# Layer 0 of a two-layer convolution and attention kernel: image sums, image loads and spectra steps in another place

## The chip, the cores and the metric

One core of a Trainium2 chip runs the whole kernel. A core has TensorE (matrix products, PE in the profile, its weight loads PEld), VectorE (DVE), ScalarE (ACT), GpSimd (POOL) and SyncE (SP, here only issuing DMAs), each with its own stream of instructions, joined by semaphores. The metric is the device time of one execution in microseconds, lower is better: the median of several runs. Everything is float32.

## The reference, cut to what matters

The input is x, 4 x 32 x 128 x 128: four "images" b, each of T = 32 planes of 128 x 128. Two layers follow each other; the change touches layer 0 alone.

```python
x = x + conv_attention(group_norm(x))       # layer 0
t = tokens(x)                               # layer 1
t = t + attention(layer_norm(t)); t = t + experts(layer_norm(t))

def conv_attention(x, ...):                 # planes xa = x.reshape(B*T, 1, H, W)
    xn = inorm(xa)                          # mean and variance of each plane
    k, q, v = fno(xn, K..), fno(xn, Q..), fno(xn, V..)   # 32 heads each
    p_attn = softmax(k and q over the T planes)
    p = fno(p_attn applied to v, P..)
    a = inorm(p + xa); an = inorm(a)
    m = gelu(inorm(spectral_conv(an)) + skip(an))
    m = inorm(spectral_conv(m)) + skip(m)
    return inorm(m) + a
```

`fno` is a spectral convolution (a 2-D FFT cut to 64 x 33 or 64 x 17 modes, a complex product for each mode, and the FFT back) plus a scaled copy of its input. `group_norm` takes mean and variance over groups of columns of a whole image, `inorm` over one plane. Both therefore need sums over all of an image before its spectra can be scaled.

## The kernel before, in words

**Staging.** Layer 0 keeps an image in SBUF as 128 partitions by 32 planes by 128 columns. FFTs are products with constant cosine and sine matrices. The loop `for b in range(B)` (L687) runs the back half of image b and, inside it, the front half of image b+1. Its stages in order of time are:

1. the load of image b+1 (`load`, L122, called at L692): four DMAs of 512 KB, two issued from SP and two from ACT;
2. the modes, `for x0 in range(0, KX, NK)` (L751): five chunks of up to 13 mode columns. For each chunk, SP broadcasts `xb` from DRAM (L758, eight DMAs, four buffers), DVE and POOL multiply (`u`, L775 and L773), PE sums into `po` (L778). The skip products `sk` (L742) are spread among them, and ACT copies a chunk out (`rs`, L788);
3. the way back to planes (`py` L798, `four` L278), and `spectra(0, q)`: by groups of GI = 8 planes, a first step `pz` (L248), copies to `z` (`evacuate`, L188 on ACT and L190 on DVE), the second step `px` (L871);
4. the first scale chain, `weighed("v0", ...)`: energies on DVE end in `v_s` (L915), a product with ones gives `ms` (L314), and a chain of small DVE and ACT operations gives `r0`, `hq`, `hs0`, `hb`;
5. `back` (L288) for two halves of the planes: `y` (L297), copies `v`, `four` (L308), and for each plane a DVE operation (L941), a GELU on ACT (L944) and its statistics (L951);
6. `image_sums` of image b+1 (L320): squares on ACT, row sums `rows8` on PE (L330, the profile's `rows`), a copy `ev`, `s12` (L343, the profile's `s`), then a DVE chain with three more small products, `mg`, `bg`, `my` (`sums`, L314), to the group norm's and the plane norm's scales `gn_r`, `colg`, `n_r`, `n_s`;
7. `spectra(1, gl)` and `spectra_of_images(b+1)` (L418): `forward` (L253) calls `first_step` (L243, `pz`), then `less_mean` (L433) takes the mean off columns 0 and 128 of `z`, then the second step `px` (L263, L264) and its scaling copy `xx` (L429);
8. the second scale chain, `attention_weights(b+1)` (L487): `so` (L503), `sod` (L506), products `pa` and `pb` on DVE (L522) and POOL (L524), `sp` (L528), the scores `sc` (L540, L547), a softmax;
9. the end of image b: ACT scales `gl` (L999), POOL adds it (L1006), DVE adds `four` (L1010), SP stores (L1016).

Before the loop, a startup does stages 6 to 8 for image 0, beside `value_weights` (L462, DVE operations L469 to L479) and other weights.

**What sets the order.** In layer 0 the tile framework's scheduler fixes the order of instructions on each engine from the program and from priorities; each engine then works strictly through its list. `tc.keep_in_program_order` and `tc.add_manual_dep` constrain it. Tiles of one tag share a fixed number of buffers. PSUM has the tags `a`, `b` and `wide`, two buffers each: `pz` and `po` are of tag `a`; `px`, `py` and `four` of `b`; `y`, `m`, `so`, `sc` and, before, all products of the image sums of `wide`. Layer 1's order is written out elsewhere and depends only on layer 0's end.

**Tables.** GELU and the logarithm with the exponential lie in two sets of ScalarE's tables, and a set is loaded when the function of another comes (`ACT_TABLE_LOAD` in the profile). `inv_std` (L204) takes a logarithm (L208) and an exponential (L209) for each inverse square root, and improves the result by a Newton step (L210 to L213). `logarithms()` (L129) loads the second set ahead of need.

Of the kernel before, what the change touches and what calls it, by code (L numbers as in the profile page):

```python
# [7 lines left out]
F32 = mybir.dt.float32  # L8
AF = mybir.ActivationFunctionType
ALU = mybir.AluOpType  # L10
# [3 lines left out]
P = 128  # L14
B, T, H, C = 4, 32, 128, 128
# [3 lines left out]
GI = 8  # L19
# [60 lines left out]
NK = 13  # L80
# [28 lines left out]
def layer0(  # L109
    tc, x, kq_modes, kq_mirror, vcw, pcw, mcols, mcol0, mrows, heads, heads_row, small_row, by_p, inv_cols, dram, x1, first  # L110
):
    nc = tc.nc
# [7 lines left out]
    const, ps, images, values, modes = (p.__enter__() for p in pools + right)  # L120

    def load(b):  # L122
        xt = images.tile([P, T, C], F32, name=f"x_{b}", tag="x")
        for g in range(0, T, GI):
            eng = nc.sync if g % 16 == 0 else nc.scalar
            eng.dma_start(out=xt[:, g : g + GI], in_=x[b, g : g + GI].rearrange("t w c -> w t c"))
        return xt
# [5 lines left out]
    loaded = load(0)  # L133
# [118 lines left out]

    def forward(images, c1, c2, take, change):  # L253


        n = c1.shape[1]
        z = grp.tile([P, GI, 192], F32, name="z", tag="z")
        first_step(images, z)
        change(z)
        for k in range(0, GI, 4):  # L260
            px = ps.tile([P, 4, n], F32, name="px", tag="b")
            for j in range(4):
                nc.tensor.matmul(px[:, j], z[:, k + j, :P], c1, start=True, stop=False)  # L263
                nc.tensor.matmul(px[:, j], z[:, k + j, 64:], c2, start=False, stop=True)  # L264
            take(k, px)
# [15 lines left out]
    GROUPS = range(0, T, GI)  # L281
# [28 lines left out]

    def sums(name, matrix, src):

        m = ps.tile(list(src.shape), F32, name=name, tag="wide")
        nc.tensor.matmul(m, matrix, src, start=True, stop=True)  # L314
        return m

    def one(name, n=1):
        return small.tile([P, n], F32, name=name, tag=name)

    def image_sums(b, xt):  # L320


        rows8 = ps.tile([64, 4, C], F32, name="rows8", tag="wide")
        for g in GROUPS:
# [13 lines left out]
        nc.scalar.copy(ev, rows8)  # L338
        s12 = ps.tile([P, 2, 512], F32, name="s12", tag="wide")[:, :, :T]
        for j in range(4):  # L340
            for k in range(2):
                r = slice(32 * k, 32 * k + 8)
                nc.tensor.matmul(s12[:, k, j::4], ev[r, j], ident[r, r], start=True, stop=True)  # L343
        sv = small.tile([P, 2, T], F32, name="sv", tag="pk_sq")
        nc.vector.tensor_copy(sv, s12)

        tot = one("tot", 2)
        nc.vector.tensor_reduce(tot, sv, AX.X, ALU.add)
        mg = sums("mg", group, tot)
        gm = one("gm")  # L350
# [11 lines left out]
        by_group = small.tile([P, 2, 32], F32, name="by_group", tag="by_group")  # L362
        nc.vector.tensor_copy(by_group, sums("bg", ones, both))
        n = 1 + 2 * KY
        colg = small.tile([P, 2, n], F32, name="colg", tag="colg")
        nc.vector.tensor_scalar(colg[:, 0], cols1[:, :n], gr, None, ALU.mult)
        nc.vector.tensor_scalar(colg[:, 1], cols2[:, :n], gr, None, ALU.mult)
        m128 = one("m128")
        nc.vector.tensor_scalar(m128, gm, 128.0, None, ALU.mult)

# [14 lines left out]
        nc.vector.tensor_scalar(y12, y12, 1.0 / NPIX, None, ALU.mult)  # L385
        my = sums("my", ones, y12)
        ym, yv = per_image("ym"), per_image("yv")
# [4 lines left out]
        ysc = scalars(ALU.mult, "n1_s", yr, par[:, N1W : N1W + 1])  # L392
        return by_group, colg, m128, ysc

# [23 lines left out]
    def spectra_of_images(b, xt, normed):  # L418


        _, colg, m128, ysc = normed
        n = 1 + 2 * KY
        xx = modes.tile([P, T, n], F32, name=f"xx_{b}", tag="xx")
        xd = dram.tile([T, 2, KX, KY], F32, name=f"xd_{b}")
        for g in GROUPS:

# [5 lines left out]

            def less_mean(z):  # L433
                nc.vector.tensor_scalar(z[:, :, 0], z[:, :, 0], m128, None, ALU.subtract)
                nc.vector.tensor_scalar(z[:, :, P], z[:, :, P], m128, None, ALU.add)

            forward([xt[:, g + t] for t in range(GI)], colg[:, 0], colg[:, 1], scaled, less_mean)

# [248 lines left out]
    for b in range(B):  # L687
        xt = loaded
        by_group, _, _, ysc = normed
        xd = front[2]  # L690
        if b + 1 < B:
            loaded = load(b + 1)  # L692

        ph, pr = weights
# [56 lines left out]
        for x0 in range(0, KX, NK):  # L751
# [3 lines left out]
            for i in range(4):  # L755
                xb = late.tile([P, 2, NK * KY], F32, name="xb", tag="xb")[:, :, :m]
                for r in range(2):
                    nc.sync.dma_start(  # L758
                        out=xb[:, r],
                        in_=xd[8 * i : 8 * i + 8, r, x0 : x0 + nk]  # L760
                        .rearrange("s x y -> s (x y)")
                        .unsqueeze(1)
                        .to_broadcast([8, 16, m]),
                    )
# [20 lines left out]
                if i % 2 and at_c < C:  # L785
                    skips(at_c)
                    at_c += 16
            nc.scalar.copy(rs[:, x0 : x0 + nk].rearrange("p x y -> p (x y)"), po)  # L788
        if b + 1 == B:
            for p in reversed(right):  # L790
                p.__exit__(None, None, None)
# [141 lines left out]
        nc.vector.tensor_mul(dq, dq, hs0)  # L933
        nc.vector.tensor_tensor(hb, hb, dq, ALU.add)
        gl = big.tile([P, T, C], F32, name=f"g_{b}", tag="y")
        st = grp.tile([P, T, 6], F32, name="st", tag="st")
# [20 lines left out]
        logarithms()  # L957
        if b + 1 < B:
            normed = image_sums(b + 1, loaded)
        else:  # L960
            first((ps, images))
# [684 lines left out]
```

## Time and profile before

| | |
|---|---|
| median of 3 runs | 3180.41 us (3179.98 to 3183.43) |
| the profiled execution | 3191.62 us, its span 3189.9 us |
| mean granted TensorE clock in it | 0.953 |
| busy share PE, DVE, ACT, POOL | 92%, 72%, 72%, 66% |
| layer 0, then layer 1 | 0 to about 1105 us, then to the end |
| `ms` of the first scale chain, b = 0, 1, 2 | 228.57, 486.75, 755.85 us |
| end of the last GELU | 256.8, 521.5, 783.6 us |
| end of `px` L871 of `spectra(1)` | 277.0, 543.5, 805.6 us |
| start of `so` (startup, then b = 0, 1, 2) | 66.8; 306.5, 572.6, 835.8 us |

How to read it: busy time is the union of the instructions of an engine; `PEclk` is the clock that the throttle granted TensorE, in tenths of full speed. In a timeline a row gives start, duration, engine, line, instruction, the tile written and the tiles read, their shapes and the count; the bracket is the engine's idle time before the row and who released it. A float32 product of TensorE mostly shows as two records. The chain of waits follows the work that ended last back from the last instruction. All line numbers are those of the kernel before.

### The profile page before, as it was taken

What the parts mean: (1) busy time and instruction counts of PE and PEld (TensorE: products, weight loads), DVE (VectorE), ACT (ScalarE), POOL (GpSimd) and SP (SyncE); (2) the same over time, 40 slices, a digit from 0 to 9 for tenths busy, and PEclk for the clock granted to TensorE, in tenths of its full rate; (3) what the DMA queues carried; (4) which work ended last, traced back from release to release, by engine and by line L of the source; (5) the groups of instructions that cost most, each with busy time, mean ns of one, the idle gap of its engine ahead of it and who ended that gap; (6) DMA issues with size and microseconds to landing.
All of it is one profiled execution on the core that took longest, in us unless ns stands there. A gap on an engine that the chain in (4) does not pass through costs nothing.

```text
span 3189.9 us, 53099 instructions
## 1 busy us (share of the span) xinstructions
PE 2928.7 (92%) x19634; PEld 1438.2 (45%) x19634; DVE 2290.9 (72%) x5035; ACT 2311.7 (72%) x3138; POOL 2102.7 (66%) x1831
## 2 busy tenths in 40 slices
PE   7888798798888789999999999999999999999997
PEld 5366365345546444444344443444444444444443
DVE  5876666667677566777666868866778777687887
ACT  2344243253343589998999999998999999999992
POOL 1621540460451289878788797889878889888773
PEclk6998998899898799999999999999999999999998
DMA  6301310130140211010111010011010011101000
GB/s 140 111 18 30 95 50 3 49 123 1 30 130 2 57 31 31 8 31 7 31 37 24 14 24 14 8 39 31 23 29 9 14 37 24 37 1 31 14 14 14
DMA packets 152308, 112.77 MB, mean 35 GB/s; under 512 B 36878, under 2 KB 140657, under 8 KB 151441
## 3 DMA queue, kind: packets, MB, share of 16 engines
q1 hardware_dynamic: 136209, 103.61, 12.2%
q10 hardware_dynamic: 15840, 5.77, 0.8%
q8 instruction: 155, 2.54, 0.3%
q14 instruction: 104, 0.85, 0.1%
HBM read 68.37 MB, written 20.00 MB: 28 GB/s over the span
## 4 chain that ended last, share of the span: by engine, by line
PE 61%; POOL 12%; ACT 9%; DVE 9%; issue 7%; DMA 1%; ACTq 0%; POOLq 0%; DVEq 0%; SPq 0%
PE d L1446 19%; PE po L1465 11%; PE px L1352 6%; ACT r L1496 4%; PE po L778 4%; PE n L1446 3%; POOL e L1505 3%; POOL e L1504 3%; PE pz L248 2%; PE four L308 2%; ACT e L1512 2%; PE px L871 1%; PE sk L742 1%; POOL kx L1111 1%; DVE r L1501 1%
## 5 line engine op out<-in xcount | busy, mean ns | idle before, releaser
L1501 DVE TENSOR_TENSOR r<-n,r 128x1024 f32<-128x1024 f32 (+1 forms) x1056 | 961.6, 952 | 479.0 <-PE n L1446 389.4
L1504 POOL TENSOR_TENSOR e<-r 128x512 f32<-128x512 f32 x528 | 673.2, 1275 | 268.1 <-DVE r L1501 267.6
L1496 ACT ACTIVATE r<-d 128x1024 f32<-128x1024 f32 (+1 forms) x1056 | 792.9, 802 | 67.4 <-PE n L1446 56.4
L1508 ACT ACTIVATE r<-r 128x1536 f32<-128x1536 f32 x528 | 783.6, 1484 | 16.8
L1505 POOL TENSOR_TENSOR e<-e,r 128x512 f32<-128x512 f32 x528 | 671.3, 1271 | 41.4
L1446 PE MATMUL d<-qe,ke 32*128 32x512 f32 (+3 forms) x2304 | 605.8, 602 | 39.6 <-ACT r L1496 36.5
L1465 PE MATMUL po<-e,kx 128*128 128x512 f32 (+3 forms) x1152 | 594.5, 605 | 15.6 <-POOL e L1517 15.6
L1446 PE MATMUL n<-qe,ke 32*128 32x512 f32 (+3 forms) x2304 | 606.2, 601 | 0.0
L1446 PE MATMUL n<-qf,kf 32*128 32x512 f32 (+3 forms) x2304 | 552.6, 554 | 0.0
L1446 PE MATMUL d<-qf,kf 32*128 32x512 f32 (+3 forms) x2304 | 550.2, 553 | 0.0
L1356 DVE SCALAR_TENSOR_TENSOR xc<-px,wgt,xc 128x128 f32<-128x128 f32 x1024 | 358.1, 350 | 42.2 <-PE px L1352 9.7
L1512 ACT ACTIVATE e<-e 128x512 f32<-128x512 f32 x528 | 325.8, 617 | 66.2 <-POOL e L1505 65.6
L1465 PEld LDWEIGHTS po<-e,kx 128*128 128x128 f32 x1152 | 175.5, 188 | 392.8 <-issue 306.9
L1446 PEld LDWEIGHTS d<-qe,ke 32*128 32x128 f32 x2304 | 176.5, 183 | 359.3 <-ACT r L1496 339.5
L773 POOL TENSOR_TENSOR u<-xb,gb 128x858 f32<-128x858 f32 (+1 forms) x120 | 233.1, 1968 | 139.5 <-PE po L778 128.0
L1446 PEld LDWEIGHTS d<-qf,kf 32*128 32x128 f32 x2304 | 220.2, 186 | 176.1 <-issue 163.8
L1352 PE MATMUL px<-we,x2t 128*128 128x512 f32 x512 | 264.0, 601 | 6.8 <-DVE xc L1356 6.0
L775 DVE TENSOR_TENSOR u<-xw,gb 128x858 f32<-128x858 f32 (+1 forms) x200 | 206.6, 1082 | 59.2 <-PE po L778 46.6
L885 POOL TENSOR_TENSOR spec<-part,part 128x512 f32<-128x512 f32 x16 | 24.8, 1550 | 333.4 <-ACT z L188 75.2
L1446 PEld LDWEIGHTS n<-qf,kf 32*128 32x128 f32 x2304 | 228.3, 185 | 19.2 <-issue 11.4
L778 PE MATMUL po<-u,pr 128*32 128x429 f32 (+1 forms) x1280 | 191.1, 548 | 26.8 <-DVE u L775 11.7
L524 POOL TENSOR_TENSOR pb<-xm 128x1024 f32<-128x1024 f32 x48 | 90.7, 1913 | 159.1 <-ACT xm L457 152.8
(388 smaller groups left out, 3953.9 us busy)
## 6 DMA issues: line engine op xcount, KB each, us to landing
xb<-xd SPq DMA_DIRECT2D x128, 214.5 KB
xc<-x SPq DMA_DIRECT2D x29, 512.0 KB
x<-x SPq DMA_DIRECT2D x16, 512.0 KB
qf<-qe SPq DMA_DIRECT2D x64, 128.0 KB
out<-xc SPq DMA_DIRECT2D x15, 512.0 KB
xb<-xd SPq DMA_DIRECT2D x32, 198.0 KB
gb<-gd SPq DMA_DIRECT2D x4, 1056.0 KB
x<-in_x SPq DMA_DIRECT2D x8, 512.0 KB
```

The costliest lines, as they stand in the source:

```text
L773: nc.gpsimd.tensor_tensor(u, xb, gk, ALU.mult)
L778: nc.tensor.matmul(po[32 * j : 32 * j + 32], pr[:, i, k], u[:, r], start=i == 0 and k == 0, stop=i == 3 and k == 1,)
L1352: nc.tensor.matmul(px, x2t[:, k * P : (k + 1) * P], we[:, e0 : e0 + 4], start=True, stop=True)
L1356: nc.vector.scalar_tensor_tensor(xc[:, k], px[:, e], wgt[:, k, e0 + e : e0 + e + 1], xc[:, k], ALU.mult, ALU.add)
L1446: nc.tensor.matmul(o, k, q, start=turn == 0 or g > 0, stop=turn == 1 or g > 0)
L1465: nc.tensor.matmul(sums[c, h][:, q0 : q0 + c1 - c0], kx[:, jb], e[:, c0:c1], start=jb == 0, stop=is_last and q0 > 2 * P, skip_group_check= ...
L1496: nc.scalar.activation(r[:, g], d, AF.Ln, scale=1.0 / DSCALE)
L1501: nc.vector.tensor_tensor(r[:, g], part, r[:, g], ALU.mult)
L1504: nc.gpsimd.tensor_tensor(e, r[:, 1], r[:, 2], ALU.add)
L1505: nc.gpsimd.tensor_tensor(e, e, r[:, 0], ALU.add)
L1508: nc.scalar.activation(r, r, AF.Exp, scale=-1.0)
L1512: nc.scalar.activation(e, e, AF.Exp)
```

## The change

It has four parts, with one consequence for allocation.

- `load` takes an instruction `behind`; for images 1 to 3 it is called after chunk 2 of the modes (`x0 == NK`). All four DMAs are issued from SP, ordered behind that chunk's last broadcast.
- `image_sums(b + 1)` is called right after `hb`, before the two `back` halves with the GELUs, not after them. Its products use the PSUM tags `a` and `b` instead of `wide`; `s12` becomes two tiles, copied by two operations.
- In `spectra_of_images`, `first_step` of the next group of planes is issued before `forward` of this one.
- The mean is taken off `z` by one operation on its columns 0 and 128 (`shift`, two values) instead of two (`less_mean`).

```diff
--- before.py
+++ after.py
@@ -119,11 +119,20 @@
     ]
     const, ps, images, values, modes = (p.__enter__() for p in pools + right)
 
-    def load(b):
+    def load(b, behind=None):
         xt = images.tile([P, T, C], F32, name=f"x_{b}", tag="x")
         for g in range(0, T, GI):
-            eng = nc.sync if g % 16 == 0 else nc.scalar
-            eng.dma_start(out=xt[:, g : g + GI], in_=x[b, g : g + GI].rearrange("t w c -> w t c"))
+            eng = nc.sync if behind is not None or g % 16 == 0 else nc.scalar
+            d = eng.dma_start(
+                out=xt[:, g : g + GI], in_=x[b, g : g + GI].rearrange("t w c -> w t c")
+            )
+            if behind is not None:
+                tc.add_manual_dep(
+                    d.ins,
+                    behind.ins.name,
+                    mybir.DependencyInfo(mybir.DependencyClass.NoSync, mybir.DependencyReason.DATA),
+                    reason="order",
+                )
         return xt
 
     def logarithms():
@@ -250,13 +259,10 @@
             if z.shape[2] > P:
                 evacuate(z[:, k : k + 4, P:], pz[:, :, :64], -1.0)
 
-    def forward(images, c1, c2, take, change):
+    def forward(z, c1, c2, take):
 
 
         n = c1.shape[1]
-        z = grp.tile([P, GI, 192], F32, name="z", tag="z")
-        first_step(images, z)
-        change(z)
         for k in range(0, GI, 4):
             px = ps.tile([P, 4, n], F32, name="px", tag="b")
             for j in range(4):
@@ -308,9 +314,9 @@
             nc.tensor.matmul(four, inv, v, start=True, stop=True)
             take([image(a, g, k) for k in range(4)], four)
 
-    def sums(name, matrix, src):
-
-        m = ps.tile(list(src.shape), F32, name=name, tag="wide")
+    def sums(name, matrix, src, tag="wide"):
+
+        m = ps.tile(list(src.shape), F32, name=name, tag=tag)
         nc.tensor.matmul(m, matrix, src, start=True, stop=True)
         return m
 
@@ -320,7 +326,7 @@
     def image_sums(b, xt):
 
 
-        rows8 = ps.tile([64, 4, C], F32, name="rows8", tag="wide")
+        rows8 = ps.tile([64, 4, C], F32, name="rows8", tag="a")
         for g in GROUPS:
             xx2 = grp.tile([P, GI, C], F32, name="xx2", tag="pr", bufs=6)
             nc.scalar.activation(xx2, xt[:, g : g + GI], AF.Square)
@@ -336,17 +342,18 @@
                     )
         ev = grp.tile([64, 4, C], F32, name="ev", tag="v", bufs=3)
         nc.scalar.copy(ev, rows8)
-        s12 = ps.tile([P, 2, 512], F32, name="s12", tag="wide")[:, :, :T]
+        s12 = [ps.tile([P, T], F32, name=f"s{t}", tag=t) for t in "ab"]
         for j in range(4):
             for k in range(2):
                 r = slice(32 * k, 32 * k + 8)
-                nc.tensor.matmul(s12[:, k, j::4], ev[r, j], ident[r, r], start=True, stop=True)
+                nc.tensor.matmul(s12[k][:, j::4], ev[r, j], ident[r, r], start=True, stop=True)
         sv = small.tile([P, 2, T], F32, name="sv", tag="pk_sq")
-        nc.vector.tensor_copy(sv, s12)
+        for k in range(2):
+            nc.vector.tensor_copy(sv[:, k], s12[k])
 
         tot = one("tot", 2)
         nc.vector.tensor_reduce(tot, sv, AX.X, ALU.add)
-        mg = sums("mg", group, tot)
+        mg = sums("mg", group, tot, "a")
         gm = one("gm")
         nc.vector.tensor_copy(gm, mg[:, 0:1])
         gv = one("gv")
@@ -360,13 +367,14 @@
         nc.vector.tensor_scalar(both[:, 0], of_group, gr, None, ALU.mult)
         nc.vector.tensor_scalar(both[:, 1], of_group, gs, -1.0, ALU.mult, ALU.mult)
         by_group = small.tile([P, 2, 32], F32, name="by_group", tag="by_group")
-        nc.vector.tensor_copy(by_group, sums("bg", ones, both))
+        nc.vector.tensor_copy(by_group, sums("bg", ones, both, "a"))
         n = 1 + 2 * KY
         colg = small.tile([P, 2, n], F32, name="colg", tag="colg")
         nc.vector.tensor_scalar(colg[:, 0], cols1[:, :n], gr, None, ALU.mult)
         nc.vector.tensor_scalar(colg[:, 1], cols2[:, :n], gr, None, ALU.mult)
-        m128 = one("m128")
-        nc.vector.tensor_scalar(m128, gm, 128.0, None, ALU.mult)
+        shift = one("shift", 2)
+        for k in range(2):
+            nc.vector.tensor_scalar(shift[:, k : k + 1], gm, 256.0 * k - 128.0, None, ALU.mult)
 
         gs128 = one("gs128")
         nc.vector.tensor_scalar(gs128, gs, 128.0, None, ALU.mult)
@@ -383,14 +391,14 @@
             y12[:, 1], sv[:, 0], grs, y12[:, 1], ALU.mult, ALU.add
         )
         nc.vector.tensor_scalar(y12, y12, 1.0 / NPIX, None, ALU.mult)
-        my = sums("my", ones, y12)
+        my = sums("my", ones, y12, "a")
         ym, yv = per_image("ym"), per_image("yv")
         nc.vector.tensor_copy(ym, my[:, 0])
         nc.vector.tensor_mul(yv, ym, ym)
         nc.vector.tensor_tensor(yv, my[:, 1], yv, ALU.subtract)
         yr, _ = inv_std("n1_r", yv)
         ysc = scalars(ALU.mult, "n1_s", yr, par[:, N1W : N1W + 1])
-        return by_group, colg, m128, ysc
+        return by_group, colg, shift, ysc
 
     prep_pool = tc.tile_pool(name="l0_prep", bufs=1)
     prep = prep_pool.__enter__()
@@ -418,11 +426,22 @@
     def spectra_of_images(b, xt, normed):
 
 
-        _, colg, m128, ysc = normed
+        _, colg, shift, ysc = normed
         n = 1 + 2 * KY
         xx = modes.tile([P, T, n], F32, name=f"xx_{b}", tag="xx")
         xd = dram.tile([T, 2, KX, KY], F32, name=f"xd_{b}")
-        for g in GROUPS:
+        steps = []
+        for g in (*GROUPS, None):
+            if g is not None:
+                z = grp.tile([P, GI, 192], F32, name="z", tag="z")
+                first_step([xt[:, g + t] for t in range(GI)], z)
+                nc.vector.tensor_tensor(
+                    z[:, :, ::P], z[:, :, ::P], shift.unsqueeze(1).to_broadcast([P, GI, 2]), ALU.add
+                )
+                steps.append((g, z))
+                if g == 0:
+                    continue
+            g, z = steps.pop(0)
 
             def scaled(k, px):
                 i = slice(g + k, g + k + 4)
@@ -430,11 +449,7 @@
                     xx[:, i], px, ysc[:, i].unsqueeze(2).to_broadcast([P, 4, n]), ALU.mult
                 )
 
-            def less_mean(z):
-                nc.vector.tensor_scalar(z[:, :, 0], z[:, :, 0], m128, None, ALU.subtract)
-                nc.vector.tensor_scalar(z[:, :, P], z[:, :, P], m128, None, ALU.add)
-
-            forward([xt[:, g + t] for t in range(GI)], colg[:, 0], colg[:, 1], scaled, less_mean)
+            forward(z, colg[:, 0], colg[:, 1], scaled)
 
             i = slice(g, g + GI)
 
@@ -688,9 +703,6 @@
         xt = loaded
         by_group, _, _, ysc = normed
         xd = front[2]
-        if b + 1 < B:
-            loaded = load(b + 1)
-
         ph, pr = weights
 
 
@@ -755,7 +767,7 @@
             for i in range(4):
                 xb = late.tile([P, 2, NK * KY], F32, name="xb", tag="xb")[:, :, :m]
                 for r in range(2):
-                    nc.sync.dma_start(
+                    broadcast = nc.sync.dma_start(
                         out=xb[:, r],
                         in_=xd[8 * i : 8 * i + 8, r, x0 : x0 + nk]
                         .rearrange("s x y -> s (x y)")
@@ -786,6 +798,8 @@
                     skips(at_c)
                     at_c += 16
             nc.scalar.copy(rs[:, x0 : x0 + nk].rearrange("p x y -> p (x y)"), po)
+            if x0 == NK and b + 1 < B:
+                loaded = load(b + 1, broadcast)
         if b + 1 == B:
             for p in reversed(right):
                 p.__exit__(None, None, None)
@@ -932,6 +946,8 @@
         nc.vector.tensor_scalar(hb, hb, par[:, S0 : S0 + 1], None, ALU.mult)
         nc.vector.tensor_mul(dq, dq, hs0)
         nc.vector.tensor_tensor(hb, hb, dq, ALU.add)
+        if b + 1 < B:
+            normed = image_sums(b + 1, loaded)
         gl = big.tile([P, T, C], F32, name=f"g_{b}", tag="y")
         st = grp.tile([P, T, 6], F32, name="st", tag="st")
         for a in HALVES:
@@ -955,9 +971,7 @@
                 add_attention(g)
 
         logarithms()
-        if b + 1 < B:
-            normed = image_sums(b + 1, loaded)
-        else:
+        if b + 1 == B:
             first((ps, images))
 
         glm, glv, flat = stats("gl", st)
```

The order in which the engines then get the work, as built: row sums of image b+1 stand on PE between the last `px` of `spectra(0)` and `ms` and just behind it, `s`, `mg`, `bg` and `my` among the `y`, and `my` ahead of the first `four`. On DVE the sums' chain stands between the steps of the `r0` chain and ahead of the first copy `v`. On ACT the logarithm and exponential of `n_r` stand between the first GELUs for b = 0 and 2, ahead of them for b = 1. At the startup `s`, `mg`, `bg` and `my` stand ahead of all `pz`.

## The prediction

> **What bounds the kernel now.** I read the page first: its slices, then its chain by engine.
>
> ```profile
> PEclk6998998899898799999999999999999999999998
> ...
> PE 61%; POOL 12%; ACT 9%; DVE 9%; issue 7%; DMA 1%; ACTq 0%; POOLq 0%; DVEq 0%; SPq 0%
> ```
>
> TensorE carries 61% of the chain, DMA 1%. From slice 15 the clock stays near full: that is layer 1 (1105 us to the end), which the change leaves alone. All gain or loss lies in layer 0, where the clock digit falls to 6 to 8 several times. Then PE's timeline of layer 0 (start, duration, instruction, count, idle before it and its releaser):
>
> ```profile
> 30.64 0.69 PE L314 MATMUL bg<-both,ones 128*128 128x64 f32 x2 [4.47 <-DVE both L361]
> ...
> 486.75 0.63 PE L314 MATMUL ms<-v_s,ones 128*128 128x32 f32 x2 [6.33 <-DVE v_s L915]
> 487.31 3.88 PE L297 MATMUL y<-cst,spec 32*128 32x128 f32 x64
> 493.01 2.65 PE L308 MATMUL four<-v,cst 128*128 128x512 f32 x4 [1.82 <-DVE v L190]
> ```
>
> `ms` ends the wait of the first scale chain: PE idles 6.33 us while VectorE makes `v_s`. The same wait stands before 228.57 (6.34) and 755.85 (6.33). What follows runs at half clock: 64 records of `y` take 3.88 us here, where the chain has 54 in 1.77 us at 625. The windows price it (PE, PEld, DVE, ACT, POOL busy; clock; DMA share; GB/s):
>
> ```profile
> 480.00:487.00 7.00, 0.67 (x10) 0.40 (x6) 6.30 (x13) 1.01 (x2) 2.17 (x1) 0.78 0.00 1
> 487.00:522.00 35.00, 33.18 (x180) 18.38 (x182) 22.85 (x95) 19.32 (x42) 0.00 (x0) 0.65 0.00 1
> 522.00:544.00 22.00, 21.31 (x201) 14.20 (x198) 10.25 (x53) 6.00 (x14) 1.27 (x1) 1.00 0.01 1
> 544.00:574.00 30.00, 26.61 (x212) 25.68 (x210) 19.73 (x68) 7.27 (x18) 1.27 (x1) 0.86 0.25 58
> 30.00:66.00 36.00, 33.10 (x150) 32.14 (x150) 17.72 (x63) 4.67 (x8) 0.00 (x0) 0.50 0.49 108
> ```
>
> From `ms` to the last GELU PE is nearly full, but at clock 0.65. Spectra of g (522 to 544) are PE's at full clock, the x spectra (544 to 574) lose 3.4 us idle and then clock, and the startup (30 to 66) never warms. Last, the chain at the load of the next image:
>
> ```profile
> 375.90 9.80 DMA xb<-xd
> ```
>
> The only long DMA step: `xb` broadcasts beside the load.
>
> **What the skill says.** "TensorE: Matmul & The Clock Gate", What's actually happening: half clock after an idle window of about 3.4 us, full after a busy one. The gaps of 6.33 us agree; but 30 to 66 shows 33 of 36 us busy at 0.50, so a busy record is not enough to warm. The table at that page's head gives the other engines strict FIFO queues: what stands behind a waiting instruction waits too, which the trace fits (`both` L361 behind 1.27-us operations). "ScalarE: Activation LUTs", What ACT_TABLE_LOAD costs: 1.28 us plus a drain, about 2.66 in all; the trace's load takes 1.28 (494.09) with the next ACTIVATE right behind it at 495.38. "DMA: Bandwidth & Descriptors", Issuing engines are not separate DMA queues: four loads on SP instead of two and two move no fewer bytes; 366 to 400 shows both queues together at up to 295 GB/s.
>
> **The change part by part**, from the order in which each engine gets its instructions, b = 0, 1, 2 for the image whose back half runs.
>
> *Row sums into the wait.* 16 products of `rows` at 0.43 us are 6.9 us, 14 of which (6.0) now stand between the last `px` and `ms`; the wait is 6.33. So `ms` moves by 0 to +0.3, PE should stay warm. They leave the GELU stage and the 2.8 us after it (b=1: 521.5 to 524.3).
>
> *The sums' vector work.* At 525 to 536 it runs from `s` to `my`, some 25 small operations of 0.15 to 0.30 us. Now it stands ahead of the first `v` copy (L190) on DVE, and `my` ahead of the first `four` on PE. First STT (L941) now comes 7.2 to 7.4 us after `ms`; interleaved with the `r` chain, whose own ACT waits hide part, I get 8.9: +1.6. Unhidden it would be 25 by 0.17, about +4. The Ln and the Exp of `n_r` (L208, L209) fall between GELUs for b = 0 and 2: four extra table loads each, 4 by 1.28 = 5.1 us (10.6 at the page's price, 0 if ACT's idle time covers them: 3.7-us gaps exist at 512). For b=1 they stand before the GELUs' own load.
>
> Before, last GELU minus `ms`: 28.2, 34.8, 27.8. The 34.8 is the cold image; DVE and ACT alone give about 28. After: 28 + 1.6 − 2 (clock, from the 3.88 against 1.8 for `y`) + 5.1 − 0.7 = 32 for b = 0 and 2, and 28 + 1.6 − 2 = 27.6 for b=1. Spectra of g then had 20.2, 22.0, 22.0 us to their last `px` L871. Without the row remainder (2.8) and `s`, `mg`, `bg`, `my` (1.8), and with more `pz` of g already issued between the `four`, 20 `pz` products (0.26, two records each) and 48 `px` products (0.11 to 0.17) remain, 11.5 us, and I say 12.5 with evacuations. Sum from `ms`: 48.4 to 44.5, 56.7 to 40.1, 49.8 to 44.5: −4, −16.5, −5.3, together **−26** (−12 to −34).
>
> *Spectra one group ahead; mean by one operation.* 64 `px` products (L263 and L264) at 0.223 are 14.3 us, the `pz` left 7.5 to 9: 23 against 29 to 30. Idle times of 1.32, 1.40 and 0.53 us (at 547.6, 565.4, 572.6) are covered by the next group's `pz`, and the second `ms` pair, which put PE behind DVE at 559 to 565, now stands after the last `px`. −5.5 each, **−16.5** (−9 to −20). The 32 TENSOR_SCALARs of 0.22 become 16 and a small one each image: DVE, hidden behind PE.
>
> *Scores.* `so` to `sc` is 38 us, set by POOL's `pb` (1.9 each) and four `x` adds (L1006, 2.35). The change moves DVE's correction chain for those adds between `pa`/`pb`; POOL's third add may wait for it. I take +2 each, **+6** (−12 to +15).
>
> *Accumulators.* The sums' products leave the `wide` tiles for tags `a` and `b`, two tiles each, which `pz`, `px` and `four` use: one of two is held from `s` to the copy of `sv`, at most the 1.2 us from 525.7 to 526.9 once an image, inside the figures above.
>
> *Load behind chunk 2.* Before, the first two chunks of modes lose about 1.5 (b=1) and 2.5 us (b=2) against 14.4 a chunk: −4 if the load is hidden. Behind chunk 2's last broadcast, 2 MB at 290 GB/s take 7 us; chunk 3's broadcasts queue behind on SP, but four buffers of 3.6 us each let them land 10.8 us before use. I give back 2: **−2** (−4 to +10). Image 0's loop lost nothing that I can price apart. ACT's two issues (1.13 us) go off ACT.
>
> *Startup.* Before, `pz` fill PE to 26, then 4.47 idle before `bg`, all `px` cold at 0.43 a product, `so` at 66.8. Now `s`, `mg`, `bg`, `my` come first; `my` stands behind some 6.8 us of value weights on DVE (0.77 to 1.27 each, L469 to L479), so about 31.4, and PE idles from 22. Then 16 `pz` products without a stop: 8 us cold (3.98 for eight at 40.85). If that warms the clock, the rest (24 more `pz`, 64 `px`) follows at 0.13 a record and 0.223 a product and `so` comes at 57.7, **−9**; if not, at 75.6, +9. For: at 822 seven cold `pz` warmed it. Against: eight at 40.85 did not. I take warm, 60 to 40.
>
> *Sum:* −26 −16.5 +6 −2 −9 = −47.5. Against the profiled execution's own 3191.6 (span 3189.9) that is 3144; that execution is 11.2 us above the median of 3180.4, and I apply the difference to the median: **3133**.
>
> **Rivals.** *(a) The startup stays cold*, the rest as above: +18 on the sum, −29.5, 3151. For it: `px` at 92% busy never warms by itself. *(b) New waits take the place of the old:* the first `four` behind `my` lets PE idle over 3.4 us again, PE is cold through the GELUs, table loads at 2.66. Then the GELU term shrinks to about −3, −3, −3 and spectra to −9, startup +9 or −9: −10 to −15, 3168. For: y's two evacuations now wait behind the sums; against: `y` itself (1.9 us of records) fills PE meanwhile. *(c) Slower: the scores stage becomes DVE's.* If POOL's third add (in front of the last `pb`s) waits for the correction chain and this for the `pa`, `so` to `sc` grows. It decides once it exceeds 38 + 47.5/3, about 54 us; at 58 it gives +12, 3193. For: POOL works strictly in order and 33.9 of 37 us are busy; against: the chain's small DVE operations stand only some 22 us after `sod`. *(d) The load stalls chunk 3*, 5 us in each of three images: −2 becomes +13, 3148. *(e) Nothing comes of it*, PE's wait being covered elsewhere: 3180; against it, the chain passes through the gap.
>
> **Numbers.** Likeliest (with d's milder forms) 0.45; a 0.25; d 0.08; b 0.09; e 0.04; c 0.09. Only what differs by over 0.2% (6.4 us) can be told from no change. Faster 0.87, same 0.04, slower 0.09. The likeliest case's own range is 3115 to 3148; with a, d and most of b, 3112 to 3170.
>
> **What would show it.** Right: no idle before `ms` in b = 0 to 2; clock near 0.9 and more from `ms` to the last GELU; `so` 10 to 22 us sooner after `ms`; `so` to `sc` still 36 to 42; `px` of the startup at 0.22 a product. Wrong: PE idle over 3 us before the first `four`; windows of the GELUs still at 0.65; the `xb` broadcasts of the third chunk named as releasers of PE's idle time; POOL idle before L1006.

## The result, and the profile after

The changed kernel is slower: 3203.22 us (median of 4 runs, 3198.16 to 3209.47) against 3181.92 us before, a ratio of 1.0067 with an interval of 1.0045 to 1.0089. That is 21 us where 47 fewer were forecast.

The page of the changed kernel, the row that answers to the first one shown of before: TensorE's granted clock in 40 slices.

```profile
PEclk8898899799898799999999999999999999999998
```

The clock is better in the startup (first digit 8 against 6) and a little worse in later slices; its mean over the first 1120 us is 0.88 in both profiles. So the clock doesn't explain the loss. (The chain of waits of this profile could be followed back only to 542.78 us, so its shares can't be set beside those of before.) In what follows a line of a profile carries the line numbers of its own kernel. PE's timeline shows that the wait before `ms` is really gone:

```profile
497.65 0.41 PE L320 MATMUL ms<-v_s,ones 128*128 128x32 f32 x2 [0.38 <-DVE v_s L929]
...
505.31 0.66 PE L320 MATMUL bg<-both,ones 128*128 128x64 f32 x2 [1.93 <-DVE both L368]
507.56 0.66 PE L320 MATMUL my<-y,ones 128*128 128x64 f32 x2 [0.44 <-DVE y L393]
508.88 3.78 PE L314 MATMUL four<-v,cst 128*128 128x512 f32 x4
```

0.38 us of idle time stand where 6.33 were. But PE now waits 1.93 us before `bg`, the first `four` starts 11.2 us after `ms`, behind `my` (493.01 − 486.75 = 6.3 before), and its four records take 3.78 us where they took 2.65 before: TensorE is cold again, at a mean clock of 0.70 in the first window below. The windows of the same image, b = 1 (the sums and `y`, the GELUs, the x spectra):

```profile
498.00:510.00 12.00, 8.99 (x91) 6.27 (x91) 9.09 (x57) 2.99 (x10) 0.00 (x0) 0.70 0.01 2
510.00:531.00 21.00, 18.77 (x130) 11.78 (x132) 18.14 (x73) 18.39 (x40) 0.00 (x0) 0.93 0.00 1
...
541.00:566.00 25.00, 22.46 (x200) 21.89 (x196) 15.71 (x41) 6.67 (x14) 1.27 (x1) 1.00 0.23 53
```

Full clock in the x spectra, 25 us instead of 30. The loss is in what follows, the scores of image 2. VectorE, GpSimd and TensorE there, first VectorE:

```profile
568.01 1.23 DVE L219 TENSOR_TENSOR r_t<-r 128x32 f32<-128x32 f32 x1 [1.77 <-ACT r L218]
569.27 1.83 DVE L220 TENSOR_TENSOR r_t<-r_t,r_ve 128x32 f32<-128x32 f32 x1
...
571.23 1.20 DVE L521 TENSOR_TENSOR sod<-ident,so 32x1024 f32<-32x1024 f32 x1
...
572.46 1.20 DVE L537 TENSOR_TENSOR pa<-xp,xm 128x1024 f32<-128x1024 f32 x1
...
601.49 0.83 DVE L1006 TENSOR_TENSOR cq<-cq,dq 128x32 f32<-128x32 f32 x1
```

Then GpSimd:

```profile
578.04 3.78 POOL L539 TENSOR_TENSOR pb<-xm 128x1024 f32<-128x1024 f32 x2 [6.99 <-PE sp L543]
...
605.62 2.36 POOL L1020 TENSOR_TENSOR x<-x,g 128x1024 f32<-128x1024 f32 x1 [3.35 <-ACT g L1013]
607.94 3.78 POOL L539 TENSOR_TENSOR pb<-xm 128x1024 f32<-128x1024 f32 x2
```

And TensorE:

```profile
572.49 1.91 PE L555 MATMUL sc<-sod,qk 32*32 32x512 f32 x2 [4.45 <-DVE sod L521]
...
594.85 1.00 PE L543 MATMUL sp<-pa,w_re 128*32 128x512 f32 x2 [2.72 <-DVE pa L537]
```

The second scale chain (`r1`, `rm`, `c2`, `cq`, from L216 to L1006) now runs inside the scores, one or two small operations between every two `pa`. `sod` waits behind its first Newton step (PE idle 4.45 us), later `pa` are late (2.72), and GpSimd waits for `sp` to give buffers back (6.99). Many of the small operations take 0.8 to 2.0 us instead of 0.17 to 0.28. A second path runs through the end of the chain: `cq`, its last result, is ready at 602.3, ACT scales `gl` with it, and only then can GpSimd's first add `x` start (605.62, after 3.35 us without work), with the last pair of `pb` behind it. In the second profile of before, which the next paragraph introduces, the adds of this image start 6.4 us after `so` and stand between the `pb`; here the first starts 39.8 us after it.

The kernel before was profiled a second time (b_again, below), at 3175.90 us, nearer its median than the first profile. Against that profile, stage by stage, in us for b = 0, 1, 2 (all line numbers of before):

| stage | before, second profile | after | sum of the changes |
|---|---|---|---|
| startup, to the first `po` | 114.1 | 111.9 | −2.2 |
| first `po` to last `px` of `spectra(0)` | 107.8, 108.1, 110.7 | 111.5, 111.9, 113.0 | +9.7 |
| that to `ms` | 6.3, 6.3, 6.3 | 6.6, 6.4, 6.6 | +0.6 |
| `ms` to last `px` of `spectra(1)` | 48.2, 47.3, 46.9 | 46.5, 43.5, 44.4 | −8.0 |
| that to `so` | 29.8, 29.1, 27.1 | 24.6, 24.6, 24.2 | −12.7 |
| `so` to the end of `sc` | 39.8, 40.8, 40.6 | 53.8, 54.8, 51.2 | +38.6 |
| `sc` to the next first `po` | 24.4, 25.6, 23.2 | 24.6, 25.5, 23.3 | +0.2 |
| image 3 to the end of layer 0 | 202.8 | 205.5 | +2.7 |

Layer 0 ends at 1114.2 instead of 1085.4, 28.8 later, which is the sum of the column but for rounding. Layer 1 takes 2084.4 against 2088.8, so the two profiles differ by less, 24 us. One row, the scores, is larger than the whole loss.

### The profile page after: what moved, and what is told of

Its sections match the earlier page's. It is cut to its first block, busy times and chain, and to the rows that moved or that the text cites. A ratio compares the mean times of both kernels' runs of the same rounds, so it can differ in the third digit from the quotient of the medians.

```text
span 3198.6 us, 53082 instructions
## 1 busy us (share of the span) xinstructions
PE 2919.1 (91%) x19634; PEld 1418.0 (44%) x19634; DVE 2309.8 (72%) x5027; ACT 2321.7 (73%) x3146; POOL 2102.3 (66%) x1831
## 3 DMA queue, kind: packets, MB, share of 16 engines
q1 hardware_dynamic: 142449, 106.75, 12.6%
q8 instruction: 155, 2.54, 0.3%
## 4 chain that ended last, share of the span: by engine, by line
PE 49%; POOL 11%; ACT 9%; DVE 7%; issue 7%; SPq 0%; DMA 0%; POOLq 0%; DVEq 0%; ACTq 0%
PE d L1460 18%; PE po L1479 10%; PE px L1366 5%; ACT r L1510 5%; PE n L1460 3%; POOL e L1519 3%; POOL e L1518 3%; PE po L790 2%; ACT e L1526 2%; POOL kx L1125 2%; DVE r L1515 2%; DVE xc L1370 1%; POOL x L1125 1%; PE pz L257 1%; PE four L314 1%
## 5 line engine op out<-in xcount | busy, mean ns | idle before, releaser
L787 DVE TENSOR_TENSOR u<-xw,gb 128x858 f32<-128x858 f32 (+1 forms) x200 | 205.8, 1081 | 68.5 <-PE po L790 57.9
L1460 PEld LDWEIGHTS n<-qf,kf 32*128 32x128 f32 x2304 | 228.2, 185 | 18.6 <-issue 11.2
L899 POOL TENSOR_TENSOR spec<-part,part 128x512 f32<-128x512 f32 x16 | 24.8, 1551 | 313.6 <-DVE part L896 115.7
```

The costliest lines, as they stand in the source:

```text
L1460: nc.tensor.matmul(o, k, q, start=turn == 0 or g > 0, stop=turn == 1 or g > 0)
```

## The experiments

Ratios are to the kernel before, run on the same chip; the edits are shown shortened. The theory, A: the scores are slow because the second scale chain was pushed in among `pa` and `pb`, and it was pushed there by the spectra one group ahead, which put the second pair of `ms` behind the last `px`. The rivals: the load, the table loads, or GpSimd's own order.

**The chain ahead of the spectra (e_chain).**

```diff
         spec, sq = spectra(1, gl)
-        if b + 1 < B:
-            front = spectra_of_images(b + 1, loaded, normed)
         v1 = weighed("v1", sq, squares, layers[1][2])
...
         nc.vector.tensor_tensor(cq, cq, dg, ALU.add)
         if b + 1 < B:
+            front = spectra_of_images(b + 1, loaded, normed)
             weights = attention_weights(b + 1, front)
```

> The changed kernel with one block of the program moved: the second scale chain (both ms products, r1, rm, c2, c3, cq) is written ahead of spectra_of_images instead of behind it. Its small VectorE operations then stand ahead of pa and pb, not between them. Theory A (the gain was eaten because this chain went in between pa and pb): so to the end of sc falls from 53.8, 54.8 and 51.3 us to 40 to 42 (40.6 before); so itself up to 3 us later in each image; total 3203 - 33 = about 3170. Rival B (the scores are slow for another reason, POOL's own order or the loads): so to sc stays above 50 and the total stays within 8 us of 3203.

Measured: 3174.64 us, ratio 0.9986 (0.9974 to 0.9998); `so` to the end of `sc` 38.4, 42.0 and 41.9 us. VectorE around `so` in this kernel:

```profile
300.70 0.18 DVE L1004 TENSOR_TENSOR cq<-cq,dq 128x32 f32<-128x32 f32 x1
...
308.43 1.21 DVE L521 TENSOR_TENSOR sod<-ident,so 32x1024 f32<-32x1024 f32 x1 [0.86 <-PE so L519]
309.86 3.49 DVE L537 TENSOR_TENSOR pa<-xp,xm 128x1024 f32<-128x1024 f32 x3 [0.22 <-ACT xp L510]
```

The chain's last operation is done 7.5 us before `sod` (3.4 and 4.0 in the next two images), and the `pa` follow each other. Nothing was taken out of the kernel, so the place of one chain accounts for 0.81% (1.0067 to 0.9986), some 26 us. A holds. The scores alone gained 37.6; part goes back in the stage ahead of them, which took 27.7, 36.3 and 24.1 us to `so` instead of 24.6, 24.6 and 24.2.

**The spectra not ahead (e_spectra).**

```diff
-        for g in (*GROUPS, None):
-            if g is not None:
+        for g in GROUPS:
...
-                steps.append((g, z))
-                if g == 0:
-                    continue
-            g, z = steps.pop(0)
```

> The changed kernel without its third part: first_step of a group directly ahead of its own forward, as before the change; the rest stays. Theory A (issuing spectra one group ahead pushed the second ms pair behind the last px, and with it the chain into pa and pb): so to the end of sc back to about 41, the x spectra back from 24 to about 29 us; per image -13 +5, total about 3203 - 24 = 3179. Rival B (the order of the scores comes from the image sums or the loads): so to sc stays above 50 and the x spectra's loss adds 15, total about 3218.

Measured: 3177.34 us, ratio 0.9992 (0.9981 to 1.0004); `so` to the end of `sc` 42.6, 40.8 and 39.8. So it is this third part of the change that moved the chain. The part lost 0.75%, about 24 us, although it made the stage of the x spectra some 5 us shorter each time (24.6, 24.6 and 24.2 against 29.7, 29.3 and 28.9).

**The load at its old place (e_load).**

```diff
-            if x0 == NK and b + 1 < B:
-                loaded = load(b + 1, broadcast)
...
+        if b + 1 < B:
+            loaded = load(b + 1)      # at the head of the image loop
```

> The changed kernel with the load back at the head of the image loop, on two queues. Theory A (the load behind chunk 2 makes chunk 2 and the start of chunk 3 wait, 2.5 to 3 us an image): first po to py falls from 71 to 68.3 us for the first three images, total 3203 - 8 = about 3195. Rival B (the modes were lengthened by something else, the load is hidden in both places): within 3 us of 3203.

Measured: 3195.86 us, ratio 1.0056 (1.0034 to 1.0077). First `po` to `py` is 67.5, 68.6 and 67.7 us, against 70.7, 71.8 and 71.5 in the changed kernel, so the stage does what A says, 10 us in all. The total moved by 0.11%, 3.5 us, inside both intervals: this run alone doesn't settle the size. In the changed kernel ScalarE's timeline shows the way it costs:

```profile
138.15 0.58 ACT L779 COPY xw<-xb 128x429 f32<-128x429 f32 x1 [3.83 <-DMA xb<-xd]
...
142.03 0.51 ACT L800 COPY rs<-po 128x429 f32<-128x429 f32 x1
```

And TensorE's:

```profile
142.59 0.91 PE L790 MATMUL po<-u,pr 128*32 128x429 f32 x2 [2.73 <-ACT rs L800]
```

Chunk 3's broadcasts, issued behind 2 MB of image, come late: ACT waits 3.83 us for one. Their copies `xw` stand ahead of chunk 2's `rs` in ScalarE's order, so `rs` is late, and PE waits 2.73 us for its accumulator.

**The load alone (b_load)**, the same edit of `load` and of its call, in the kernel before.

> The kernel before with the third part of the change alone: all four loads on SP behind the last broadcast of chunk 2. Theory A (the broadcasts of chunk 3 stand behind 2 MB on SP, ACT's copies of them stand ahead of the copy of chunk 2): first po to the last px of spectra(0) longer by 2 to 3 us for b = 0, 1, 2, total 3178 + 7 = 3185. Rival B (the stall only comes with the rest of the change): within 3 us of 3178, or below it since the loss of the first two chunks is gone.

(The expectation calls the load the third part; in the list of the change it is the first.) Measured: 3182.08 us, ratio 1.0005 (0.9993 to 1.0017). First `po` to last `px` is 110.3, 111.6 and 110.9 us: +2.5, +3.5 and +0.2 on the second profile of before, 6.2 in all. But the first `po` of this profile comes at 108.1, not 114.1, which gives 6 us back. Two things come together there. One is the clock of the startup: TensorE's timelines at the same place, first the kernel before,

```profile
40.85 3.98 PE L248 MATMUL pz<-cst,x 128*128 128x128 f32 x16 [1.20 <-ACT z L188]
45.10 0.67 PE L263 MATMUL px<-colg,z 128*128 128x67 f32 x2 [0.27 <-DVE xx L429]
```

then b_load.

```profile
41.10 3.98 PE L257 MATMUL pz<-cst,x 128*128 128x128 f32 x16 [1.20 <-ACT z L197]
45.35 0.41 PE L272 MATMUL px<-colg,z 128*128 128x67 f32 x2 [0.27 <-DVE xx L438]
```

The same rows, the same 3.98 us, and in one of them the clock is full afterwards; `so` starts at 57.1 instead of 67.2. Whether the edit has a part in that (fewer bytes move at the startup) or chance decides it, no run here tells. The clock alone doesn't bring the first `po` forward, though: e_best2 (below) is as warm (`so` at 58.8) and has it at 113.8. Its load of image 1 is at the old place, and there SP issues half of it right ahead of the first broadcasts:

```profile
87.07 1.05 SPq L126 DMA_DIRECT2D x<-in_x  x2
88.23 5.74 SPq L783 DMA_DIRECT2D xb<-xd  x8
...
95.51 0.52 ACT L792 COPY xw<-xb 128x429 f32<-128x429 f32 x1 [33.61 <-DMA xb<-xd]
```

In b_load nothing stands ahead of them:

```profile
85.32 9.05 SPq L765 DMA_DIRECT2D xb<-xd  x10
...
89.13 0.52 ACT L774 COPY xw<-xb 128x429 f32<-128x429 f32 x1 [28.66 <-DVE energy L664]
```

The first copy `xw` starts 7.3 us after the first broadcast is issued in the one, 3.8 us in the other. Over all profiles, e_spt apart, which alters just this place, the first `po` follows that issue by 21.6 to 23.1 us where the load was moved (six profiles) and by 25.0 to 27.5 where it was not (seven). So the move loses time in the modes and gains some 2 to 6 us at the startup. In the stage A holds for b = 0 and 1; in the total (1.6 us by the ratio, −2.2 to +5.4 by its interval) B does.

**The plane scale after the GELUs (e_nr).**

```diff
-        yr, _ = inv_std("n1_r", yv)      # in image_sums
...
         logarithms()
+        if b + 1 < B:
+            normed = plane_scales(normed)   # n_r by Ln and Exp, n_s
```

> The changed kernel with the last step of the image sums (the plane scale n_r, its Ln and Exp) done after the GELUs, as before the change; all sums stay in the early place. Theory A (four more table loads between the first GELUs delay b = 0 and 2): two table loads an image again, last GELU 4 to 5 us earlier after ms for b = 0 and 2, none for b = 1, total 3203 - 9 = about 3194. Rival B (ACT has slack there, PE or DVE set the end of the GELU stage): last GELU moves by less than 2 us, total within 4 us of 3203.

Measured: 3197.99 us, ratio 1.0063 (1.0039 to 1.0087), last GELU 36.1 and 34.7 us after `ms` for b = 0 and 2 (36.0 and 37.2 in the changed kernel). The expectation's premise was not met: the scheduler put Ln and Exp, now together, in the middle of the GELUs, so three extra loads were left of four (at 249.94, 251.49 and 254.00 for b = 0). One of them stands between Ln and Exp, so the table that is loaded for Ln here does not serve Exp; where `logarithms()` loads one ahead, it serves both. The run says little on the price; e_best2 below says more.

**Chain ahead and load at its old place (e_chain_load)**, the two edits above together.

> The changed kernel with the second scale chain written ahead of the spectra of the next image, as in e_chain, and the load back at the head of the image loop. If the two add up: 3174.6 - 7 = about 3167. If the chain's gain had already covered the load's stall: within 2 us of 3174.6.

Measured: 3167.59 us, ratio 0.9956 (0.9938 to 0.9975), 0.30% or 9 to 10 us below e_chain, whose interval begins at 0.9974: as forecast if the two add up. It doesn't settle the load's price. First `po` to `py` fell by only 2.1, 0.2 and 0.6 us between these two profiles, and 11.4 us of their difference lie in one stretch of x spectra, 36.3 us long in e_chain and 24.9 here. The three pairs that differ in the place of the load give 3.5 us (e_load), 9 to 10 (here) and 1.6 (b_load). What all profiles agree on is the stage: first `po` to last `px` of `spectra(0)`, summed over b = 0, 1, 2, is 4.3 to 12.7 us longer than in the second profile of before in the five with the whole load behind chunk 2, and −1.0 to +1.5 in the six others with it at the old place.

**And no table load between GELUs (e_best2).**

```diff
         ln = nc.scalar.activation(r, ve, AF.Ln)      # in inv_std, for n_r
+        tc.add_manual_dep(ln.ins, last_gelu.ins.name, NoSync, reason="order")
```

> As e_chain_load, and the Ln of the plane scale n_r ordered behind the last GELU, so that each image has two table loads and none between GELUs. Theory A (the extra loads set the end of the GELU stage for b = 0 and 2): last GELU 4 to 5 us earlier after ms there, total about 8 us below e_chain_load, 3159. Rival B (DVE, PE or the copies set it): within 3 us of e_chain_load.

Measured: 3163.82 us, ratio 0.9950 (0.9931 to 0.9969). The last L941 comes 34.2, 30.9 and 30.2 us after `ms`, against 36.7, 35.5 and 36.0 in e_chain_load: 2.5 and 5.8 us for b = 0 and 2. The 4.5 us of b = 1 aren't the tables', since neither kernel has a load between its GELUs there (and in e_spt, below, with the same loop, it takes 36.6). The medians differ by 3.8 us, and the intervals overlap. The extra loads cost time in their stage; how much of it reaches the end is not resolved. ScalarE in the changed kernel, to show them:

```profile
243.18 1.28 ACT L960 ACT_TABLE_LOAD   x1
...
244.99 1.28 ACT L217 ACT_TABLE_LOAD   x1
246.28 0.23 ACT L217 ACTIVATE n_r<-n_r_ve 128x32 f32<-128x32 f32 x1
246.53 1.28 ACT L960 ACT_TABLE_LOAD   x1
```

**Only the sums early, their chain late (e_rows2).**

```diff
             nc.vector.tensor_copy(sv[:, k], s12[k])
+        return sv                     # early: squares, rows, s, sv
+
+    def rest_of_sums(sv):             # after the GELUs, Ln behind the last of them
         tot = one("tot", 2)
```

> As e_chain_load, but only squares, row sums, s and the copy sv are early; tot, mg, gn_r and all that follows are written after the GELUs, their Ln behind the last GELU. Theory A (the sums' vector chain ahead of the first v and my ahead of the first four made the first L941 wait 12.7 us after ms): first L941 at ms + 7 to 8, last GELU about 5 us earlier than in e_best2, spectra of g up to 2 us longer, total 3 to 9 us below e_best2, about 3153. Rival B (what is taken from there comes back between the last GELU and the x spectra, which need colg): total within 3 us of e_best2 or above.

Measured: 3186.24 us, ratio 1.0023 (1.0013 to 1.0033), 22 us above e_best2. The first L941 does come at `ms` + 8, the last at 28.8, 24.8 and 25.8; but the last `px` of `spectra(1)` comes at 53.4, 50.1 and 52.9 (42.9, 41.9 and 47.7 in e_best2). What the GELUs gain is more than lost where `mg`, `bg` and `my` come after them. B holds: the early chain costs at the first `four` and is still the right place.

**The kernel before again (b_again)**, unchanged.

> The kernel before, unchanged, profiled a second time. The first profile took 3191.6 us where the median of its runs is 3180. Theory A (that profile caught an unusual clock state: the stage of the GELUs of b = 1 at 0.65): this one shows 26 to 29 us from ms to the last GELU for b = 1, as for b = 0 and 2, not 34.8, and a time of 3175 to 3185. Rival B (the profiler's own constant cost): again about 34.8 us there, and about 3191.

Measured: 3175.90 us. `ms` to the last GELU is 27.9, 25.3 and 24.8 us. TensorE at the GELUs of b = 1:

```profile
484.88 0.63 PE L314 MATMUL ms<-v_s,ones 128*128 128x32 f32 x2 [6.34 <-DVE v_s L915]
485.44 4.14 PE L297 MATMUL y<-cst,spec 32*128 32x128 f32 x64
491.14 1.99 PE L308 MATMUL four<-v,cst 128*128 128x512 f32 x4 [1.56 <-DVE v L190]
```

The wait and the cold `y` are the same, but the clock is back for `four` (1.99 us against 2.65). A holds: the 34.8 us of the first profile belong to that execution. In the comparisons of b_load and the runs beside it the kernel before took between 3171 and 3192 us.

**The sums alone (e_only_sums)**: load and spectra as before, sums early, one operation for the mean.

> The image sums in the early place and the mean taken off by one operation, without the other parts: the load at the head of the loop, each group's first step directly ahead of its own forward. Theory A (of the change the sums gain a little: ms to the last px of spectra(1) 46.5, 43.6, 44.4 us against 48.2, 47.3, 46.8 in the second profile of the kernel before; the startup nothing to 2): 3178 - 8 = 3170. Rival B (the sums themselves cost, through the table loads and the late first L941): 3178 or more.

Measured: 3172.11 us, ratio 0.9973 (0.9964 to 0.9981), 8.6 us faster. These two parts of the change together gain by themselves.

**The startup's copy first (e_spt)**, in e_best2.

```diff
                     d = nc.scalar.copy(xw[:, r], xb[:, r])
+                    if b == 0 and x0 == 0 and i < 2:
+                        tc.add_manual_dep(d.ins, spt_copy[0].ins.name, NoSync, reason="order")
```

> e_best2 with ACT's copy spt of the startup ordered ahead of the copies xw of image 0's first broadcasts. Theory A (at the startup only ACT's order holds the scores: spt stands behind xw, which wait for broadcasts that SP issues at 89 us): sc starts 5 us earlier at the startup, first po at 108 to 109, total 3163.8 - 5 = 3159. Rival B (the broadcasts themselves bound the first po): sc earlier, first po within 1 us of 113.8, total within 2 us of e_best2.

Measured: `sc` at 89.6 instead of 97.8, first `po` at 108.5 instead of 113.8; 3165.61 us, ratio 0.9943 (0.9921 to 0.9965). The stage does what A says, with 5.3 us; the total can't be told from e_best2's. (Moving the load away from the startup gains as much there: e_best_split2, below, has its first `po` at 108.8.) In the changed kernel ScalarE's timeline has the wait that it takes away:

```profile
94.86 0.52 ACT L779 COPY xw<-xb 128x429 f32<-128x429 f32 x1 [1.56 <-DMA xb<-xd]
95.31 0.58 ACT L551 COPY spt<-sp 128x512 f32<-128x512 f32 x1
```

**One load behind each chunk (e_best_split2)**, in e_best2.

```diff
-        if b + 1 < B:
-            loaded = load(b + 1)
...
+            if b + 1 < B and x0 < 4 * NK:
+                load_part(b + 1, loaded, GI * (x0 // NK), broadcast)   # 512 KB, on SP
```

> e_best2 with the four loads of the next image one behind each of the first four chunks' last broadcasts, all on SP, where e_best2 has them together at the head of the loop. Theory A (what stalls is 2 MB in one piece; 512 KB, some 2 us, fit into the broadcasts' slack): first po to py 66 to 67 us for b = 1, 2 where e_best2 has 68, total 1 to 5 us below e_best2, 3160. Rival B (any load in front of a broadcast delays it beyond the slack): po to py above 69, total above e_best2.

Measured: 3165.02 us, ratio 0.9949 (0.9926 to 0.9971); first `po` to `py` 68.5 and 67.9 us for b = 1, 2 against 68.3 and 67.7. Neither theory: there, pieces of 512 KB cost no more than the load at the head, and gain nothing. For b = 0 the stage is 1.6 us longer (68.9 against 67.3), and the first `po` comes 5 us sooner (108.8 against 113.8), since nothing of image 1 stands ahead of the first broadcasts.

## Why the prediction was wrong

Three steps held in their mechanism. The x spectra gained −12.7 of the −16.5 forecast, at full clock. The startup's `px` did warm (`so` at 59.9 instead of 67.2), and so they did in all nine profiles with this startup (`so` at 57.8 to 60.3); the reasons given for it, one case against one, were no better than 60 to 40. The mean in one operation cost nothing visible. A fourth held by half: the rows filled the wait (0.38 us left), but the clock did not stay up, as PE then waited for `both` (1.93 us for b = 1, 2.54 for b = 0 and 2) and ran the first `four` cold. From `ms` to the last GELU the mean clock is 0.86, 0.84 and 0.86, where the second profile of before has 0.84, 0.90 and 0.91. That is the mechanism of rival (b) in a milder form; it was given 0.09.

**Scores, "+6": the step that failed.** It measured +38.6. The step took `so` to `sc` as set by GpSimd and asked only when its third add would get `cq`. It saw in the order of instructions that the chain stood between `pa` and `pb`, and priced that by the add alone; rival (c) put the chain's operations some 22 us behind `sod`, where the first of them stood ahead of it. What it left out is that those operations are queued on VectorE ahead of the `pa` and of `sod`, for which TensorE waits, and TensorE gives the buffers back for which GpSimd waits. The wait that it did ask about came too, at the first add and not the third (3.35 us, with the last `pb` behind). Both go with the chain: with it ahead of the spectra (e_chain) or with the spectra not ahead (e_spectra) the stage is back at 38 to 43 us; how the 38.6 us divide between the two, no run tells.

Also the step gave the chain's operations no duration of their own. In the three score stages of the changed kernel the small ones that overlap a GpSimd instruction last 11.9, 12.9 and 12.4 us together (11 or 12 of them), those that don't 2.4 to 2.6 (13 or 14), while the `pa`, one input of which lies in PSUM, take 1.21 in both cases. The Trainium skill has this in "SBUF — State Buffer", SBUF: two separate sides: VectorE instructions with two SBUF inputs or in a two-port mode, and GpSimd's, take turns at a shared port as an exclusive lock. The trace fits it; that the lock, and not just the place in the queue, makes the larger part of the 38.6 no run separates.

Rival (c), "the scores stage becomes DVE's", had the mechanism in the main, with 0.09. Its threshold of 54 us assumed that the rest would give 47.5, and at 48 to 49 us to the start of `sc` the change was already slower. (The 47.5 hold the +6 of the scores already: without it the rest is 53.5, the threshold 55.8, and 58 us give +6.5 and not +12.)

**Sums, "−26": mis-sized, −8.0.** Some 9 of the 26 were the 34.8 us of one execution (25.3 in the second profile); the rule that the profiled execution's 11.2 us over the median are a constant was wrong, they were layer 0's. Of the others, the first L941 came at `ms` + 12.6 to 13.3, not 8.9: `sv`, `mg`, `bg` and `my` are four round trips between VectorE and TensorE, and the sum over VectorE's durations left their latencies out. The last GELU came 36.0, 32.6 and 37.2 us after `ms` (32, 27.6 and 32 forecast, with the four table loads for b = 0 and 2), and the −2 for the clock did not come. The rest of `spectra(1)` then took 10.6, 10.9 and 7.1, less than the 12.5 assumed.

**Load, "−2": wrong in sign.** +9.7 in the stage. The slack of 10.8 us was counted on the buffers; the copies `xw` that wait for late broadcasts hold back `rs` behind them on ScalarE, which the step didn't ask about. Rival (d) had it, at 5 us an image instead of 2.3 to 3.7. And the step could price nothing at image 0, where the load stood in the way of the first broadcasts: b_load shows that its move gains there what it loses in the modes, as far as the total can tell.

**Startup, "−9": −2.2.** `so` came 7.3 earlier; then `spt` waited behind `xw` for broadcasts that SP issues from 89.1 us on (88.5 and 86.6 in the two profiles of before), and `sc` ended at 101.5 (101.4 before). The gain met a chain of transfers that had not moved forward.

Corrected by these, the sum is −8.0 − 12.7 + 38.6 + 9.7 − 2.2 = +25.4, and +3.5 in the rows left over. The range missed because its bounds were drawn step by step around the values taken, and the scores' upper bound, +15, was less than half of what that step cost.

## What to carry to other kernels

When a change moves small operations into a stage, ask not only what waits for their results but what is queued behind each of them on its engine, and whether that engine feeds the loop of the stage; their duration there is that beside the other engine's work, not that in the quiet place they came from. A step that makes one stage shorter can take the cover from the next: look up where the chain that used to hide in it goes. Work that is moved into a wait to keep the clock up helps only if it makes no new wait behind. And two profiles of the kernel before, if they can be had, show which of its waits and cold stretches are there every time.

## What was not expected of the hardware

- Most operations of VectorE on 128x32 that fell into GpSimd's 128x1024 products in the scores of the changed kernel took 0.75 to 1.98 us, and those without them 0.17 to 0.28.
- The clock after an idle stretch did not follow from the kernel alone: the stage of the GELUs of b = 1 took 34.8 and 25.3 us in two executions of the same kernel. And the same eight `pz` products, 3.98 us without a stop, left TensorE cold in the kernel before and warm in b_load (0.67 and 0.41 us for a pair of `px` records), worth 10 us to `so`. In e_chain PE idled 2.17 us ahead of 533.46, and the x spectra of that image (528.5 to 565) had a mean clock of 0.67, those of the next (795 to 819) 1.00.
- 2 MB in one piece behind chunk 2's broadcasts lengthened first `po` to last `px` by 0.2 to 4.7 us an image (five profiles, against the second one of before); pieces of 512 KB cost b = 1 and 2 no more than the load at the head of the loop.
